# Factorization kernel: the linear layer and the squares' product with outputs on the partitions, four of its outer products by two levels of Strassen in pairs

## The chip, the cores and the metric

The kernel runs on one core of a Trainium2 chip. The metric is the device time of one execution in microseconds (us); less is better. All data are f32.

## The reference

`x` is 1024 x 512, `weight` is 64 x 512 x 512 (e, f, m), `lin_w` is 512 x 512:

```python
out_lin = x @ lin_w.T + lin_b
xv = jnp.einsum('bf,efm->bem', x, weight)
zp = jnp.einsum('bf,efm->bem', jnp.square(x), jnp.square(weight))
interaction = 0.5 * jnp.sum(jnp.square(xv) - zp, axis=1)
return out_lin + interaction
```

The sum over e goes into the second product: the sum of `zp` over e is the product of the squares of `x` (1024 x 512) with the sum over e of the squares of `weight` (512 x 512). It is called the squares' product below. The first product, `xv`, has no such shortcut: it is 64 products of 1024 x 512 with 512 x 512, squared and summed over e.

## The kernel before

**Groups and trees.** The 512 model columns are cut into 16 groups of 32. Within a group the four quadrants of the weights are loaded (w11, w12, w21, w22a or w22b), each 512 columns wide for one quarter of the group's columns and all 64 e. The group's product is done by two levels of Strassen's scheme in Winograd's form: seven outer products, each a `tree` of seven inner ones. A `product` of a tree is two matmuls of 128x512 into one PSUM buffer (b1, b3 or one of two b2). The stationary side are sums of blocks of x, held in `x_all` (X1 to X7, seven slots each); the moving side are blocks of the weights and their sums t1 to t4, which GpSimd makes ahead of each tree. ScalarE copies PSUM to SBUF or from b1 to b2, VectorE adds PSUM to earlier blocks, `finish` squares a block on ScalarE and sums it over e on VectorE (into `acc`). `w_squares` squares the weights on ScalarE and sums them over e on VectorE into `w2_sum`. A group's finished `acc` is halved and stored to DRAM (`acc_dram`).

**The linear layer** comes first: one level of the same scheme, seven products (`lin_product`, `big_product`) of 8 matmuls of 128x256; the batch rows lie on the partitions, x is the stationary side. Its four blocks go to DRAM (`lin_dram`).

**The squares' product** comes last, with one level too: seven products (`zp_product`), x squared as the stationary side, the batch on the partitions. The blocks of x are loaded again, squared on ScalarE, and summed on GpSimd; column sums of `w2_sum` are made on GpSimd (`column_sums`). The bias (broadcast over the partitions), the linear blocks and the groups' sums are loaded and accumulated by DMA into four output blocks, `add_part` adds the products from PSUM with a factor of -0.5, `add_edge` adds the last group's own sums, and each block is stored.

**The order.** `Plan` collects every operation with a cost per engine and what it reads and writes. The order on TensorE is given by keys: a tree s has key 7 s plus a place for each of its products:

```python
PLACE = {5: -6, 3: -2, 1: 0, 6: 3, 2: 4, 7: 6, 4: 9}
```

so that products of three neighbouring trees alternate (in the steady state 1, then 5 of the next tree, 4 of the one before, 6, 2, 3 of the next, 7). From these keys each operation gets a latest time, and `order` runs a list schedule over ScalarE, VectorE, GpSimd and SyncE: an engine takes the ready operation whose latest time comes first, and does not start one that would hold up a more urgent one. Loads and stores are issued by SyncE at most `AHEAD = 50.0` us before their latest time; a DMA is planned with 0.45 us of issue, its `move` time on a shared wire, and 2.0 us to land; GpSimd's accumulating ones with 0.9, a longer move, and 2.5. The result is a fixed order of instructions on each engine; the engines take them in that order and wait for each other by semaphores.

Of the kernel before, what the change touches and what calls it, by code (L numbers as in the profile page):

```python
# [29 lines left out]
class Plan:  # L30
# [10 lines left out]
    AHEAD = 50.0  # L41

# [5 lines left out]
    def add(self, costs, emit, reads=(), writes=(), key=None, land=0.0,  # L48
            move=0.0, both=False):
        op = SimpleNamespace(  # L50
            n=len(self.ops), costs=costs, emit=emit, key=key, land=land, move=move,
            deps=set(), succ=[], latest=None, end=None, both=both, engine=None,
        )
        for r in reads:
            if r in self.writer:
                op.deps.add(self.writer[r])
        for w in writes:
            op.deps.update(self.readers[w])
            if w in self.writer:
                op.deps.add(self.writer[w])  # L60
        for r in reads:
            self.readers[r].append(op.n)
        for w in writes:
            self.writer[w], self.readers[w] = op.n, []
        op.deps.discard(op.n)
        self.ops.append(op)
# [124 lines left out]
def kernel(  # L191
# [33 lines left out]

    nc = tc.nc
    NG, NQ, _, NCB, KH, N = weight.shape
    B = xT.shape[1]
    M = out.shape[1]
# [49 lines left out]
    acc_ring = ring("acc", 2, [P, NB, MG])  # L279
    w2_sum = sb.tile([P, NK, M], F32, tag="w2_sum", name="w2_sum")  # L280
    acc_dram = dram.tile([P, NB, M], F32, tag="accd", name="accd")
    lin_dram = dram.tile([P, NB, M], F32, tag="lind", name="lind")

    plan = Plan()
    engines = {DVE: nc.vector, POOL: nc.gpsimd}
    PAIR = 1.72
# [70 lines left out]
    for at, k in enumerate((2, 3, 0, 1)):  # L357
        load_x(1, k, 0, 2, 10.0 + 0.8 * at)
    nc.scalar.preload_act_table(AF.Square)
# [50 lines left out]
    def quarter(ap):  # L410

        return ap.rearrange("p a (b m) -> p (a b) m", b=2)

# [12 lines left out]
    def big_product(bank, lhs, rhs, first, keys, by_k=False):  # L426

        (a, a_names), (b, b_names) = lhs, rhs
        steps = [(u, [k]) for k in range(KH) for u in range(G)]
        for (u, ks), key in zip(steps if by_k else [(u, range(KH)) for u in range(G)], keys):  # L430
            def emit(_, u=u, ks=ks):
                for j in range(2):
                    for k in ks:
                        nc.tensor.matmul(  # L434
                            buf[bank][:, u, ts(j, HM)],
                            a[:, k, ts(2 * u + j, P)],
                            b[:, k, :],
                            start=first and j == 0 and k == 0,
                            stop=k == KH - 1,
                            skip_group_check=True,  # L440
                        )

            names = a_names + b_names
            if by_k:
                names = sum((a_names[2 * k + u:2 * k + u + 1] + b_names[k:k + 1] for k in ks), ())
            plan.add({PE: PAIR * len(ks) / KH}, emit, names + ((bank, u),), ((bank, u),), key=key)
# [20 lines left out]
    def lin_product(p, bank, first, key, last=None, by_k=False):  # L467
        keys = [key, last or key + 0.2, key + 0.4, key + 0.6]
        big_product(bank, lhs[p], rhs[p], first, keys, by_k)

    def lin_store(n, h, c):
        dma(lin_dram[:, ts(h, NB // 2), ts(c, HM)], quarter(buf[n]), (n,), (("lind", h, c),))

    def lin_last(n, bank, sign):

        def emit(_):
            if sign > 0:
                nc.vector.tensor_add(buf[n], buf[bank], buf[n])
            else:
                nc.vector.scalar_tensor_tensor(  # L480
                    buf[n], buf[n], -1.0, buf[bank], ALU.mult, ALU.subtract
                )

        reads = both_halves(bank) if bank.startswith("b") else (bank,)
        plan.add({DVE: 1.14}, emit, (n, *reads), (n,))

    lin_product(1, "b2_1", True, -1000, by_k=True)
    act(buf["ob2"], buf["b2_1"], None, both_halves("b2_1"), ("ob2",))
# [4 lines left out]
    act(buf["c_0"], buf["b2_0"], None, both_halves("b2_0"), ("c_0",))  # L493
    lin_product(5, "b3", True, -997)
    act(buf["c_1"], buf["b3"], None, both_halves("b3"), ("c_1",))
    lin_product(6, "b2_1", False, -996)
    act(buf["ob3"], buf["b2_1"], None, both_halves("b2_1"), ("ob3",))
    lin_product(3, "b3", False, -995)
    act(buf["c_2"], buf["b3"], None, both_halves("b3"), ("c_2",))
# [19 lines left out]
    def used(*names):  # L519

        plan.add({SP: 0.0}, None, (), names, land=-plan.HOP)

    for n in tuple(a_buf.values()) + ("ob0", "ob1"):
        used(n, *((n, r, u) for r in range(KH) for u in range(2)))
    for b in ("b1", "b3", "b2_0", "b2_1"):
        used(b, *both_halves(b))
# [158 lines left out]
    for g in range(NG):  # L685
# [7 lines left out]
        for idx, i in enumerate(order):  # L693
# [8 lines left out]
            if i == 5:  # L702
                w_squares(g, "w22")
            tree(7 * g + idx, g, i, order)
        if g + 1 < NG:
            names = tuple((acc_name[g], *k) for k in acc_parts)
            a = buf[acc_name[g]]
            plan.add({ACT: 0.4}, lambda _, a=a: nc.scalar.mul(a, a, 0.5), names, names)
            dma(acc_dram[:, :, ts(g, MG)], buf[acc_name[g]], names, names + (("accd", g),), 0.9)


    for n in ("w11", "w12", "T2", w(NG, "w22")):
        for c in range(2):
            buf[n, c] = buf[n][:, c]
        used(n, (n, 0), (n, 1))
    for b in ("b1", "b3", "b2_0", "b2_1"):
        used(b, *both_halves(b))
    last = acc_name[NG - 1]
    blocks = [(h, c) for h in range(2) for c in range(2)]
    lin_all = dict(zip(blocks, ((n, c) for n in ("T2", w(NG, "w22")) for c in range(2))))  # L720
    xe = dict(zip(blocks, ((n, c) for n in ("w11", "w12") for c in range(2))))
    for (h, q), n in xe.items():
        dma(buf[n], x_src[:, ts(q, KH), ts(h, H)], (), (n,))
    edge = {0: HM, 1: HM - MG}
    for h, c in blocks:
        n, rows = lin_all[h, c], ts(h, NB // 2)
        for j in range(NB // 2):
            dma(quarter(buf[n])[:, j, :], lin_b[ts(c, HM)].partition_broadcast(P), (), (n,), 0.5)
        load_more(n, lin_dram[:, rows, ts(c, HM)], (("lind", h, c),), 2.7, quarter)
        load_more(n, acc_dram[:, rows, c * HM:c * HM + edge[c]],  # L730
                  tuple(("accd", x) for x in range(NG - 1)), 2.7,
                  lambda ap, w=edge[c]: quarter(ap)[:, :, 0:w])
    for n in xe.values():
        act(buf[n], buf[n], AF.Square, (n,), (n,), 1.07)

    place = {5: 1, 6: 6, 7: 2, 3: 7}
    lhs = {p: (buf[xe[b]], (xe[b],)) for p, b in ((1, (0, 0)), (2, (0, 1)), (4, (1, 1)))}
    a21 = (buf[xe[1, 0]], (xe[1, 0],))
    for p, a, b, kind in (
        (5, a21, lhs[4], "a + b"),  # L740
        (6, 5, lhs[1], "a - b"),
        (7, lhs[1], a21, "a - b"),
        (3, lhs[2], 6, "a - b"),
    ):
        i = place[p]
        a, b = (lhs[z] if isinstance(z, int) else z for z in (a, b))
        lhs[p] = (block4(i), (f"R{i}",))
        x_sum((f"R{i}", f"X{i}", f"Y{i}"), block4(i), a[0], b[0], kind, a[1] + b[1], 1024, POOL)
    w2_quad = [w2_sum[:, ts(q, KH), ts(c, HM)] for q in range(2) for c in range(2)]
    w2_names = [  # L750
        tuple(("w2", q, m) for m in range(c * HM, (c + 1) * HM, MI))
        for q in range(2) for c in range(2)
    ]
    zt_place = dict(zip(range(1, 5), place.values()))
    zt = {k: x_all[:, i - 1, 4:6, :] for k, i in zt_place.items()}
    zt_names = {k: (f"X{i}", ("zt", k)) for k, i in zt_place.items()}
    column_sums(POOL, w2_quad, zt, w2_names, zt_names)
    rhs = {1: (w2_quad[0], w2_names[0]), 2: (w2_quad[2], w2_names[2]),
           3: (w2_quad[3], w2_names[3])}
    rhs.update({p: (zt[k], zt_names[k][1:]) for p, k in ((4, 4), (5, 1), (6, 2), (7, 3))})  # L760

    def add_edge(h):

        n = lin_all[h, 1]
        l = quarter(buf[n])[:, :, edge[1]:HM]
        a = buf[last][:, ts(h, NB // 2), :]
        plan.add(
            {DVE: 0.3},
            lambda _: nc.vector.scalar_tensor_tensor(l, a, 0.5, l, ALU.mult, ALU.add),
            (n,) + tuple((last, i, pos) for i in ((2, 3), (4, 5))[h] for pos in range(4)), (n,),  # L770
        )

    out_dst = out.rearrange("(n p) m -> p n m", p=P)
    last_key = 7 * (7 * NG - 1) + PLACE[4]
    bank_a, bank_2, bank_b, bank_3 = "b1", "b2_0", "b2_1", "b3"

    def add_part(h, c, bank, store, piece=None):

        n = lin_all[h, c]
        tiles = piece or (0, 4)  # L780
        o = quarter(buf[n])[:, tiles[0]:tiles[1], :]
        b = quarter(buf[bank])[:, 0:tiles[1] - tiles[0], :]
        name = (n, piece) if piece else n
# [81 lines left out]
```

## Time and profile before

| | before |
|---|---|
| median of 3 runs (lowest to highest), us | 1405.06 (1404.98 to 1405.61) |
| profiled execution, us | 1405.08 |
| its span, us | 1403.3 |
| granted TensorE clock | 0.999 |
| TensorE busy, us (share), records | 1398.5 (100%), 3364 |
| VectorE / ScalarE / GpSimd busy, us | 1082.3 / 692.5 / 1037.4 |
| DMA, mean over the span | 141 GB/s |

The span goes from the first to the last instruction of the profiled execution; the execution's own time is 1.8 us longer. PE is TensorE's matmuls, PEld its weight loads, DVE VectorE, ACT ScalarE, POOL GpSimd, SP SyncE; a trailing q is an engine's issuing queue. An f32 matmul leaves two records. L608 is the line of the trees' matmul, L434 that of the linear layer and of the squares' first six products, L820 that of its last.

### The profile page before, as it was taken

What the parts mean: (1) busy time and instruction counts of PE and PEld (TensorE: products, weight loads), DVE (VectorE), ACT (ScalarE), POOL (GpSimd) and SP (SyncE); (2) the same over time, 40 slices, a digit from 0 to 9 for tenths busy, and PEclk for the clock granted to TensorE, in tenths of its full rate; (3) what the DMA queues carried; (4) which work ended last, traced back from release to release, by engine and by line L of the source; (5) the groups of instructions that cost most, each with busy time, mean ns of one, the idle gap of its engine ahead of it and who ended that gap; (6) DMA issues with size and microseconds to landing.
All of it is one profiled execution on the core that took longest, in us unless ns stands there. A gap on an engine that the chain in (4) does not pass through costs nothing.

```text
span 1403.3 us, 10560 instructions
## 1 busy us (share of the span) xinstructions
PE 1398.5 (100%) x3364; PEld 639.8 (46%) x3364; DVE 1082.3 (77%) x934; ACT 692.5 (49%) x719; POOL 1037.4 (74%) x706
## 2 busy tenths in 40 slices
PE   9999999999999999999999999999999999999998
PEld 7444444444444444444444444444444444444446
DVE  7977696867859687696867869687696867869676
ACT  3545463544636355463544636455463544636442
POOL 4796776958678596776958678596777958678694
PEclk9999999999999999999999999999999999999999
DMA  6572562917538183562917548282572907447365
GB/s 228 161 196 75 135 180 77 237 38 186 148 103 200 53 221 91 138 184 77 232 36 188 145 105 198 56 223 85 142 183 79 230 33 191 143 109 198 87 122 118
DMA packets 54551, 197.57 MB, mean 141 GB/s; under 512 B 19168, under 2 KB 30688, under 8 KB 32608
## 3 DMA queue, kind: packets, MB, share of 16 engines
q0 software_dynamic: 15312, 84.81, 31.4%
q1 hardware_dynamic: 38624, 111.55, 22.7%
q8 instruction: 28, 0.46, 0.1%
q10 hardware_dynamic: 560, 0.52, 0.1%
q14 instruction: 27, 0.22, 0.0%
HBM read 173.93 MB, written 6.16 MB: 128 GB/s over the span
## 4 chain that ended last, share of the span: by engine, by line
PE 100%; DVE 0%; issue 0%
PE b L608 96%; PE b L434 3%; PE b L820 0%; PE b L364 0%; DVE w22a L786 0%
## 5 line engine op out<-in xcount | busy, mean ns | idle before, releaser
L608 PE MATMUL b<-t,x_all 128*128 128x512 f32 x1792 | 805.9, 592 | 0.0
L608 PEld LDWEIGHTS b<-t,x_all 128*128 128x128 f32 x1792 | 340.4, 190 | 427.9 <-issue 420.5
L608 PE MATMUL b<-w,x_all 128*128 128x512 f32 x768 | 358.1, 592 | 0.0
L294 POOL TENSOR_TENSOR t<-w 128x512 f32<-128x512 f32 x128 | 173.2, 1354 | 156.1 <-PE b L608 85.0
L306 ACT COPY p<-b 128x1024 f32<-128x1024 f32 x161 | 162.0, 1006 | 161.8 <-PE b L608 161.8
L608 PEld LDWEIGHTS b<-w,x_all 128*128 128x128 f32 x768 | 145.9, 190 | 183.3 <-issue 172.4
L294 POOL TENSOR_TENSOR t<-w,t 128x512 f32<-128x512 f32 x128 | 175.7, 1373 | 61.6 <-PE b L608 61.6
L308 ACT ACTIVATE oa<-oa 128x1024 f32<-128x1024 f32 x124 | 129.7, 1057 | 139.0 <-DVE oa L294 137.1
L608 PE MATMUL b<-T,x_all 128*128 128x512 f32 x384 | 180.4, 592 | 0.0
L315 DVE TENSOR_REDUCE acc<-oa 128x16 f32<-128x1024 f32 x124 | 149.2, 1213 | 37.8 <-ACT oa L308 37.8
L306 ACT COPY b<-b 128x1024 f32<-128x1024 f32 (+1 forms) x114 | 113.1, 992 | 122.9 <-PE b L608 120.1
L315 DVE TENSOR_REDUCE w_sum<-wsq 128x16 f32<-128x1024 f32 x128 | 154.9, 1212 | 20.7 <-ACT wsq L308 20.7
L294 DVE TENSOR_TENSOR oa<-b,p 128x1024 f32<-128x1024 f32 x95 | 116.0, 1221 | 37.7 <-PE b L608 37.6
L294 POOL TENSOR_TENSOR t<-T 128x512 f32<-128x512 f32 x64 | 90.6, 1415 | 58.0 <-issue 33.2
L308 ACT ACTIVATE wsq<-w 128x1024 f32<-128x1024 f32 x96 | 98.1, 1056 | 69.1 <-DVE w_sum L315 69.1
L308 ACT ACTIVATE c<-c 128x1024 f32<-128x1024 f32 x68 | 70.1, 1056 | 93.0 <-POOL c L294 62.2
L608 PEld LDWEIGHTS b<-T,x_all 128*128 128x128 f32 x384 | 73.0, 190 | 91.8 <-issue 91.6
L294 DVE TENSOR_TENSOR ob<-b,p 128x1024 f32<-128x1024 f32 x48 | 58.7, 1222 | 68.2 <-PE b L608 68.2
L294 DVE TENSOR_TENSOR p<-b,p 128x1024 f32<-128x1024 f32 x79 | 96.4, 1220 | 17.5 <-PE b L608 17.4
L294 POOL TENSOR_TENSOR t<-T,t 128x512 f32<-128x512 f32 x64 | 81.3, 1270 | 18.9 <-PE b L608 18.9
L294 POOL TENSOR_TENSOR ob<-ob,p 128x1024 f32<-128x1024 f32 x32 | 89.8, 2815 | 0.0
L294 POOL TENSOR_TENSOR c<-oa,p 128x1024 f32<-128x1024 f32 x32 | 88.6, 2767 | 0.0
(86 smaller groups left out, 1392.8 us busy)
## 6 DMA issues: line engine op xcount, KB each, us to landing
w<-weight SPq DMA_DIRECT2D x48, 1024.0 KB, 4.9
T<-weight POOLq DMA_DIRECT2D x45, 1024.0 KB, 8.6
T<-weight SPq DMA_DIRECT2D x30, 1024.0 KB, 7.1
w<-weight POOLq DMA_DIRECT2D x16, 1024.0 KB, 11.2
w<-T POOLq DMA_DIRECT2D x16, 1024.0 KB, 7.0
w22a<-weight SPq DMA_DIRECT2D x8, 1024.0 KB, 8.1
w22b<-weight SPq DMA_DIRECT2D x8, 1024.0 KB, 8.1
w<-xT SPq DMA_DIRECT2D x4, 512.0 KB, 4.8
```

The source lines that it names most:

```text
L294: f(o, a, b)
L306: nc.scalar.copy(o, i)
L308: nc.scalar.activation(o, i, func)
L315: lambda _: nc.vector.tensor_reduce(o, i.rearrange("p a (m e) -> p a m e", e=E), axis=AX.X, op=ALU.add),
L434: nc.tensor.matmul(buf[bank][:, u, ts(j, HM)], a[:, k, ts(2 * u + j, P)], b[:, k, :], start=first and j == 0 and k == 0, stop=k == KH - 1, ...
L608: nc.tensor.matmul(buf[b][:, j, :], buf[f"X{i}"][:, SLOT[p], ts(j, P)], op, start=first, stop=True, skip_group_check=True,)
```

## The change

1. **Linear layer.** The stationary side are now blocks of `lin_w`, the moving side blocks of x, so that model columns lie on the partitions. The bias becomes a 128x4 tile with one value a partition, and is added when ScalarE copies the products from PSUM (`lin_copy`).
2. **Groups' sums.** A group's `acc` is halved, turned in 32x32 blocks by a VectorE transpose (`turn`) and stored with the model columns on the partitions, by four DMAs (`place`). There is one `acc` buffer instead of two, and one `turned`.
3. **Squares of x.** In groups 1 to 7, one of the seven outer blocks of x squared is made in each (`x_squares`): loads, squares, sums on VectorE, stored to `sq_dram`; for blocks 1, 2, 5 and 6 with the sums of their inner level.
4. **Squares' product.** Outer products 1 and 2, and 5 and 6, are done in pairs by a second level (`twin_tree`): for each of seven inner products, two matmuls of 128x256, one for each member, into the two halves of a PSUM buffer. The first pair stands in the last group's sequence, between its fifth and its sixth tree; the second follows the last tree. Products 4, 7 and 3 stay at one level (`one_level`), on top of an earlier block that ScalarE puts into PSUM (`preload`). Their keys put parts of product 4 between the last tree and the second pair. The last group squares w22 two trees earlier.
5. **End.** Output blocks have model columns on the partitions and are stored in pieces from SyncE or ScalarE; the kernel's output is transposed on the way out (a view). The last group's own sums reach their partitions by DMAs within SBUF before `add_edge`.

The diff, cut to its core:

```diff
-    acc_ring = ring("acc", 2, [P, NB, MG])
+    acc_ring = ring("acc", 1, [P, NB, MG])
+    make("turned", [P, NB, MG])
+    bias = sb.tile([P, M // P], F32, tag="bias", name="bias")
...
+    nc.scalar.dma_start(bias[:], lin_b)
+    landing("bias", 9.5)
...
-    def big_product(bank, lhs, rhs, first, keys, by_k=False):
+    def lin_product(p, bank, first, key, last=None, by_k=False):
+        (a, a_names), (b, b_names) = lhs[p], rhs[p]
+        for at, key in enumerate((key, last or key + 0.2) + (key + 0.4, key + 0.6) * by_k):
+            if by_k:
+                k, u = divmod(at, 2)
+                steps = [(k, c, slice(u * Q, (u + 1) * Q)) for c in range(2)]
...
+            else:
+                steps = [(k, at, slice(0, H)) for k in range(KH)]
...
+                    nc.tensor.matmul(
+                        buf[bank][:, c, rows], b[:, k, ts(c, P)], a[:, k, rows],
...
+    def lin_copy(n, bank, c, sign):
+        for u in range(2):
+            plan.add({ACT: 0.56}, lambda _, u=u: nc.scalar.activation(
+                    buf[n][:, u, :], buf[bank][:, u, :], AF.Identity,
+                    bias=bias[:, 2 * c + u:2 * c + u + 1], scale=sign,
...
+    def turn(g, tiles, half=True):
...
+            plan.add({ACT: 0.2 + 0.25 * size}, lambda _: nc.scalar.mul(a, a, 0.5), row, row)
+        plan.add({DVE: 0.1 + 0.27 * size}, lambda _: nc.vector.transpose(
...
+    def place(dst, b, names, writes, move):
+        rows = dst.rearrange("m (n q b) -> q m n b", q=P // MG, b=MG)
+        for q in range(P // MG):
+            dma(rows[q], buf["turned"][ts(q, MG), b, :], names, (writes + (q,),), move)
+
+    def x_squares(i):
+        a, b = c_ring(), c_ring()
...
+                dma(buf[o], x_src[:, ts(q, KH), ts(h, H)], (), (o,))
+                act(buf[o], buf[o], AF.Square, (o,), (o,), 1.07)
+        one, two, kind = {
+            1: ("A11", None, None), 2: ("A12", None, None), 4: ("A22", None, None),
+            5: ("A21", "A22", "a + b"), 6: (5, "A11", "a - b"), 7: ("A11", "A21", "a - b"),
+            3: ("A12", 6, "a - b"),
+        }[i]
...
+            x_sum((a,), buf[a], buf[a], buf[b], kind, (a, b), 1024)
+        if i in raw_dram:
+            dma(raw_dram[i], buf[a], (a,), (("rawd", i),))
+        slots = sq_dram[:, i - 1, 0:4, :].rearrange("p (k q) b -> p k (q b)", k=2)
+        if i in (3, 4, 7):
+            return dma(slots, buf[a], (a,), (("sqd", i),))
...
+            x_sum(to, o, x, y, kind, (a, b), Q)
...
-            if i == 5:
+            if i == (5 if g < NG - 1 else 2):
                 w_squares(g, "w22")
+            if idx == 1 and 0 < g < 8:
+                x_squares((1, 2, 4, 5, 6, 7, 3)[g - 1])
+            if idx in before:
+                before[idx]()
+            tree(7 * g + idx + sum(idx >= b for b in before), g, i, order)
...
+    def square_load(i):
+        names = (f"R{i}", f"X{i}", f"Y{i}")
+        dma(buf[f"X{i}"], sq_dram[:, i - 1], (("sqd", i),), names, 3.1)
...
+    def twin_tree(at, b2, members):
+        bank = {n: buf[n][:, :, 0:Q] for n in ("b1", "b3", b2)}
...
+        def product(p, b, first):
+            for u, (i, _, _) in enumerate(members):
+                op, names = tt[i][p]
+                plan.add({PE: PAIR / 4}, lambda _, u=u, i=i, op=op: nc.tensor.matmul(
+                        bank[b][:, u], op, buf[f"X{i}"][:, SLOT[p], :], start=first, stop=True,
...
+                    key=7 * at + PLACE[p] + 0.1 * u,
...
+        product(5, "b3", True)
+        aside(5, 3)
+        product(3, "b3", False)
+        aside(3, 1)
+        product(1, "b1", True)
+        act(bank[b2], bank["b1"], None, ("b1",), (b2,), 0.65)
+        product(6, b2, False)
+        to(1, b2, 3)
+        product(2, "b1", False)
+        to(0, "b1")
+        product(7, b2, False)
+        to(3, b2, 5)
+        product(4, b2, False)
+        to(2, b2)
...
+    group(last, {5: first_twins})
...
+            one_level(4, upper[u], u, q * Q, (q + 1) * Q, ((-0.6, -0.4), (9.5, 6.4))[q][u])
...
+    twin_tree(S, b2, ((6, v, u2), (5, None, f)))
+    for h in (1, 0):
+        b, names = turn(last, 1 + h, h == 1)
+        place(buf["oa2"][P - MG:P, h, :], b, names, ("edge", h), 0.0)
     add_edge(1)
...
+        one_level(7, (b2, u), u, 0, H, 11 - u)
...
+            one_level(3, bank, u, q * Q, (q + 1) * Q, 14 - 2 * u + q)
+            collect((0, 1), bank, u, q * Q, (q + 1) * Q)
+        if u:
+            add_edge(0)
+        for q in range(2):
+            store(0, 1, (2 * q + u,))
```

In `twin_tree`, `to` takes an inner product's result out of PSUM (one 128x512 operation for the first pair; one of 128x256 for each member of the second), and `aside` keeps those of b3 in SBUF, with earlier blocks added on GpSimd where a member has them. `S` is 113, the place after the last tree; the first pair has 110, between trees 109 and 111. `first_twins` also starts the loads of the linear blocks and of the groups' sums, and scales `w2_sum` by -0.5 (`halve`).

## The prediction

> **What bounds the kernel now.** I read the page first. TensorE (PE) is busy for 1398.5 of 1403.3 us, VectorE (DVE) 77%, GpSimd (POOL) 74%, ScalarE (ACT) 49%, at a granted clock of 0.999. Then the chain of work that ended last, in order of time:
>
> ```profile
> 3.68 4.52 PE b L434 x16
> 8.20 0.02 issue
> 8.22 19.34 PE b L434 x88
> 27.56 1.72 PE b L608 x4
> 29.27 1.73 PE b L434 x8
> 31.00 1342.43 PE b L608 x3128
> 1373.43 3.45 PE b L434 x16
> 1376.89 1.72 PE b L608 x4
> 1378.60 17.27 PE b L434 x80
> 1395.87 3.47 PE b L820 x16
> 1399.34 0.02 issue
> 1399.36 0.42 DVE w22a L786
> ```
>
> The columns are start, length, what. PE never stands still between 0.78 and 1399.34, so the time is PE's work plus 3.96 us from its last matmul to the end of the span (1403.3). Each f32 matmul leaves two records: 3128 records in 1342.43 us are 0.4292 us each, so a 128x512 matmul of the trees (L608) costs 0.858 us. The last product's three groups (L434 late, L820) are 112 records, 56 matmuls of 256 columns, in 3.45 + 17.27 + 3.47 = 24.19 us: 0.432 us each. Only two things can move the time: fewer columns through PE, or a stop of PE, for which the waits of ACT between 31 and 1372 us show what the present order leaves open:
>
> ```profile
> ACT p L306 <- PE b L608: 159.4, 54, 5.9
> ...
> ACT wsq L308 <- DVE w_sum L315: 69.1, 18, 4.7
> ```
>
> Each line gives who waited for whom, the total, how often, the longest. ACT's list, and DVE's beside it, name no DMA as a releaser at all: the squares of the weights (wsq) are fed by loads, and none came late. The rows of DMA issues (size, median us to landing) price what the change adds:
>
> ```profile
> w<-weight SPq DMA_DIRECT2D x48, 1024.0 KB, 4.9
> ...
> w<-xT SPq DMA_DIRECT2D x4, 512.0 KB, 4.8
> accd<-acc SPq DMA_DIRECT2D x15, 128.0 KB, 6.3
> ...
> out<-w22a SPq DMA_DIRECT2D x2, 128.0 KB, 2.1
> ```
>
> **Part 1: PE's work, on the path.** Before, the seven products of the squares are 56 matmuls of 256 columns, 24.19 us. After, four of them (1, 2, 5, 6) run as two pair trees of 7 products x 2 members, 28 matmuls of 256 columns; products 4 and 3 are 8 such matmuls each; product 7 is 4 matmuls of 512. That is 44 x 0.432 + 4 x 0.858 = 22.44 us, 1.75 us less. In the linear layer the weights become the stationary side; five of its seven products go from 40 matmuls of 256 to 20 of 512: 17.28 - 17.17 = 0.11 us less. The first two keep 16 of 256 and the same loads in the same order, so the beginning (where PE takes 25.59 us for 56 x 0.432 = 24.19) stays. PE: **-1.86 us**, its last matmul at about 1397.5. That is the whole prize: 0.13% of the time.
>
> **Part 2: the linear layer's copies, off the path.** Each 1.01 us ACT copy becomes two halves with bias and scale (the 128x512 copy took 0.57): 1.14. The tightest user is product 3 on b3, which comes one product (3.45 us) after product 5. The bias is 2 KB on ACT's queue behind three loads; the load in front of it was issued at about 2 us and took 6.5, so bias lands near 9, when product 1 has just ended (8.20), and its bank is needed again only after three more products. Cost 0. ACT's in-order queue holds the next copy of x behind that first bias copy, at most 1 us, against over 10 us until the trees use it.
>
> **Part 3: the squares of x, in groups 1 to 7.** Eleven 512 KB loads, 9 squares on ACT (1.06 each), 4 DVE sums of 128x1024 and 16 of 128x256, and 13 stores are moved from the end into the groups, past the queues of SP, ACT and DVE. The DVE prices, alone and beside POOL: a 128x1024 sum took 1.18 us at 13.68 us, where POOL was idle; the groups of DVE sums by shape (busy us, mean ns, idle before) give it beside POOL, and the small one:
>
> ```profile
> L294 DVE TENSOR_TENSOR x_all<-x_all 128x256 f32<-128x256 f32 x8 | 5.4, 687 | 7.3 <-ACT x_all L306 7.3
> ...
> L294 DVE TENSOR_TENSOR T<-w,w 128x1024 f32<-128x1024 f32 x2 | 4.6, 2284 | 0.0
> ```
>
> The dearest group (5 or 6) adds 2.28 + 4 x 0.69 = 5.0 us to a DVE that is busy 64.9 of 84 us a group, and 2.1 to an ACT busy 42.2. Capacity is there; what can hurt is order. ACT and DVE take their instructions in order: an ACT square whose load is late holds every PSUM copy queued behind it. The handover it would break: product 1 ends, ACT copies b1 to b2 (1.0), and product 6 needs it two products (3.43 us) later, so about 2.0 us are free after two hops of 0.2. The order plans 0.45 + 1.75 + 2.0 + 0.3 = 4.5 us for such a load; the nearest row measured 4.8, so 0.3 late, which the 2.0 cover. Lower bound 0: a PE that is never idle has nothing to win back; upper bound, if every one of 11 were 3 us late, 11 x 1.0 = 11 us. I take 0.1, because the row is near the plan and since ACT and DVE never waited for a load.
>
> The turning of each group's sums adds one DVE transpose of 128x256. No row shows one; between the 0.28 of a 128x128 DVE op and the 1.21 of a 128x1024 reduce I take 0.4, in 19 us of idle time a group. Four stores replace one, on SP; behind them stand weight loads that SP issues up to 50 us ahead. Cost 0, and if SP were held, 50 us of lead would have to go first.
>
> **Part 4: the last group.** The squares of w22 come two trees earlier; the first pair tree stands between trees 5 and 4. Its X2 (0.9 MB) can only be loaded once tree 2's last product has gone: five products, 8.58 us, before its first use. 1 MB took 4.9 us in the row above, 8.1 in w22a's row on the page: covered, by 0.5 us in the worse case. In the last pair tree the handovers shrink: product 6 to DVE to product 7 has 0.43 + 0.86 = 1.29 us, and needs 0.2 + 0.42 (a 128x256 DVE add at 1399.36) + 0.1. It fits unless a 1.22 us DVE add stands in front, when it is 0.2 to 0.3 late; the same from 7 to 4. I take 0.1, between 0 and 0.6. POOL loses 4 sums of x (2.46 to 4.36 each at the end) and gains the inner sums (planned 3.3 twice), 8 sums of 128x256 and two asides: about even, and the first half is ready long before.
>
> **Part 5: the end.** Now the last product's DVE add (0.42) and a 128 KB store close the span: 3.96 us after PE. After, the same add and the same store do. New is a chain to the two stores before them: tree 3's last product ends 6 x 0.864 + 3.43 + 3.46 = 12.07 us before PE's end; then DVE add 1.22, square 1.06, reduce 1.21, transpose 0.4, four issues of 0.525 (accd's), the landing, and the edge add, about 0.6: 6.6 us and a landing, with some 2.5 us of hops and of DVE's pair-tree adds in front. The landing of 64 KB in 128-byte pieces lies between 1.8 (fastest 128 KB store) and 5.6 (fastest accd, 128 KB in such pieces); 3 is in between as it is half the bytes. That makes 12.1, just PE's end, so the edge's two stores and the last two crowd: 1.5 MB leave in the last 5 us, at the 342 GB/s of 1400 to 1401 us 4.4 us of transfer. Price 0 to +1.5, also -0.3 if the second issuing queue helps; I take **+0.5**.
>
> The Trainium skill ("DMA: Bandwidth & Descriptors", Why small descriptors are slow) says that the penalty of small pieces belongs to HBM, and that copies within SBUF are spared it. The edge copies are within SBUF, so by the page they would land in about 2 us (Specifications and the fit beside it give 2.0 plus bytes over 436 GB/s, an estimate), and the end would cost 0: 1403.4. No row here shows such a copy; the sum keeps its own bounds.
>
> Sum: 1405.08 (profiled execution; the median of the runs is 1405.06) - 1.86 + 0.1 + 0.1 + 0.5 = **1403.9 us**. Its own range: 1402.7 (end -0.3, no stops) to 1405.6 (end +1.5, stops 0.9).
>
> **Rivals.** *The saving is eaten at the end or in the pair trees* (15%): edge chain at +1.5 and handovers at 0.6: 1405.3. For it: VectorE is busy about 23 of the last 26 us already. Still inside what counts as no change.
>
> *Late loads stop PE* (22%): the eleven loads of Part 3, taken by in-order ACT and DVE, in groups where POOL's accumulating loads (1 MB, 8.6 to 11.2 us) share the wires. It decides from a lateness of 2.0 us. For it: w22a's loads took 8.1 us against 6.2 planned, and a 512 KB transfer of the linear sums up to 11.7. Against: no wait of ACT or DVE on DMA in 1340 us. With half of them 3 us late, 5.5 x 1.0 = 5.5 us: 1409.4, slower than now.
>
> *Much faster* (5%): the end would have to shrink by 1 us more; but 0.42 add, 0.36 issue and 1.8 of landing are in every end: about 1402.0.
>
> *The change does not do what it says*: two levels on four products must show as 3308 PE records instead of 3364 (1568 tree matmuls, 36 linear, 48 squares, 2 warm-up, times two). The code leaves no doubt of it; no chance given.
>
> **How the numbers follow.** The likeliest (58%) is 1403.9. A measurement of this kernel tells a change of about 0.2% (2.8 us) from none: faster below 1402.25, slower above 1407.87. Likeliest and first rival lie within: 0.73; late loads 0.22; much faster 0.05. The range goes from 1402.6 to 1408.6, into the late-load case until some two in ten are left out; the likeliest alone has 1402.7 to 1405.6.
>
> **What would show it.** Right: PE unbroken from 31 us to about 1397.5; 3308 records; 3.9 to 5 us from last matmul to end; no DMA among ACT's releasers in groups 1 to 7. Wrong: waits of PE's weight loads on ACT or DVE between 100 and 690 us that lengthen a group beyond 84.1 us (late loads), a gap between the first and the last pair tree, or an edge add after PE's end.

## The result, and the profile after

| | before | after |
|---|---|---|
| median of 11 runs (lowest to highest), us | 1405.61 (1404.94 to 1406.04) | **1409.2** (1408.49 to 1409.52) |
| profiled execution / span, us | 1405.08 / 1403.3 | 1409.28 / 1407.2 |
| PE's last matmul ends, us | 1399.34 | 1403.20 |
| from there to the end of the span, us | 3.96 | 4.00 |

The ratio is 1.0026, interval 1.0017 to 1.0035: slower, by a little more than the 0.2% that can be told from no change, and 0.6 us above the top of the range. The page of the kernel after:

```profile
PE 1398.1 (99%) x3308; PEld 628.9 (45%) x3308; DVE 1094.7 (78%) x976; ACT 711.8 (51%) x760; POOL 1043.1 (74%) x736
```

The 3308 records are there, so PE got the smaller work. It no longer works without a break. The chain of waits of the kernel after (start, length, what), cut, from 1381.85 us to PE's end:

```profile
1381.85 1.74 PE b L1083 x8
...
1386.24 0.38 ACT b L322
...
1386.67 1.14 PE b L938 x4
...
1388.01 0.76 DVE T L975 x2
...
1388.81 1.13 PE b L938 x4
1389.94 0.88 PE b L1083 x4
...
1390.85 0.77 DVE T L975 x2
...
1391.75 1.10 PE b L938 x4
1392.85 2.59 PE b L1083 x8
...
1395.47 0.60 ACT b L322
...
1396.11 2.00 PE b L1083 x4
...
1400.81 0.34 DVE T L1095
...
1401.19 2.01 PE b L1083 x8
```

L938 is the second pair tree, L1083 the products at one level; line numbers are those of the changed kernel. Where before had PE alone, ScalarE and VectorE now stand between its pieces, five times. PE's waits after 1383 us in the kernel after (who, for whom, total, times, longest); in the kernel before this list is empty:

```profile
PE b L1083 <- DVE T L1095: 1.4, 1, 1.4
PE b L938 <- DVE T L975: 1.1, 2, 0.9
PE b L1083 <- ACT b L322: 0.7, 1, 0.7
PE b L938 <- ACT b L322: 0.5, 1, 0.5
```

In order of time PE waits 0.52 us before product 6 of the pair tree (1386.67), 0.15 before 7 (1388.81), 0.94 before 4 (1391.75), 0.68 before the second half of outer product 7 (1396.11) and 1.37 before the last half of outer product 3 (1401.19): 3.7 us. Each time the next group is slow as well: the one at 1386.67 took 1.14 us for two matmuls of 256 columns, where the same work in an unbroken run took 0.86. Five times about 0.27 us are 1.4 more. A count of the work agrees: from 1383.41 PE had 22 matmuls of 256 columns and 6 of 512 left, 22 x 0.432 + 6 x 0.858 = 14.65 us, to 1398.06. It ended at 1403.20: **5.1 us of stops**. The expectations below count each stop from where PE at full speed would have been done with what it had, and so call the five 0.68, 0.42, 1.2, 0.84 and 1.54 us.

The timeline of the kernel after (start, busy time, operation, and in brackets the idle time before it with its releaser) shows what kind of waits these are:

```profile
1392.69 2.74 PE L1083 MATMUL b<-x_all,w 128*128 128x256 f32 x8
...
1396.11 1.98 PE L1083 MATMUL b<-x_all,w 128*128 128x512 f32 x4 [0.68 <-ACT b L322]
...
1398.19 0.69 DVE L1095 TENSOR_TENSOR w22a<-w22a,b 128x512 f32<-128x512 f32 x1 [2.14 <-PE b L1083]
```

The first half of outer product 7 was in its bank by 1395.44 (end of the group at 1392.85 in the chain). VectorE, idle for 2.14 us, adds it at 1398.19: only after the second half, in the other bank of the same buffer, has ended too (1398.11).

### The profile page after: what moved, and what is told of

Its sections match the earlier page's. It is cut to its first block, busy times and chain, and to the rows that moved or that the text cites. A ratio compares the mean times of both kernels' runs of the same rounds, so it can differ in the third digit from the quotient of the medians.

```text
span 1407.2 us, 10698 instructions
## 1 busy us (share of the span) xinstructions
PE 1398.1 (99%) x3308; PEld 628.9 (45%) x3308; DVE 1094.7 (78%) x976; ACT 711.8 (51%) x760; POOL 1043.1 (74%) x736
## 4 chain that ended last, share of the span: by engine, by line
PE 98%; DMA 1%; DVE 0%; ACT 0%; issue 0%; ACTq 0%; SPq 0%; DVEq 0%
PE b L623 96%; PE b L456 1%; PE b L938 1%; PE b L1083 1%; DMA oa<-xT 0%; DMA ob<-lin_wT 0%; ACT b L322 0%; DVE T L975 0%; DVE w22a L1095 0%; ACT T L322 0%; DVE x_all L310 0%; ACTq L356 0%; DVE T L1095 0%; SPq L349 0%; ACT ob L324 0%
## 5 line engine op out<-in xcount | busy, mean ns | idle before, releaser
L310 POOL TENSOR_TENSOR t<-w,t 128x512 f32<-128x512 f32 x128 | 176.4, 1378 | 60.4 <-PE b L623 60.4
L310 POOL TENSOR_TENSOR t<-T 128x512 f32<-128x512 f32 x64 | 90.3, 1411 | 56.6 <-issue 33.2
L324 ACT ACTIVATE c<-c 128x1024 f32<-128x1024 f32 x77 | 79.4, 1057 | 77.5 <-POOL c L310 51.7
```

The lines of the kernel that those rows point to most:

```text
L310: f(o, a, b)
L324: nc.scalar.activation(o, i, func)
```

## The experiments

**The theory:** an engine that reads one half of a PSUM buffer waits for every matmul or copy that was issued earlier into any part of that buffer, and one that writes a half waits for the earlier reads too. The plan that sets the order gives the halves names of their own (`(b, u)`, `upper`) and takes them to be independent; the semaphores, which are made from the order of the instructions, go by the whole buffer. **The rival:** ScalarE and VectorE have too much to do in the last 25 us. A third question is the first 31 us, where the kernel after is 0.5 us behind.

**1. The wait by itself.** A small kernel of its own with four cases: VectorE copies what one matmul wrote, while other matmuls go to another place. A tile is a buffer; the second number of `mm` is how many matmuls, the third their columns (512 where it is left out).

```python
    # one tile, two banks: the read of bank 0 is issued after the matmuls to bank 1
    mm(one[:, 0, :], 1)
    mm(one[:, 1, :], 6)
    nc.vector.tensor_copy(o["one"][:], one[:, 0, :])
    # two tiles
    mm(twoa[:], 1)
    mm(twob[:], 6)
    nc.vector.tensor_copy(o["two"][:], twoa[:])
    # one bank, lower and upper half
    mm(low[:, 0:256], 1, 256)
    mm(low[:, 256:512], 12, 256)
    nc.vector.tensor_copy(o["low"][:, 0:256], low[:, 0:256])
    # one tile, two banks: the read of bank 0 comes first in the program
    mm(pre[:, 0, :], 1)
    nc.vector.tensor_copy(o["pre"][:], pre[:, 0, :])
    mm(pre[:, 1, :], 6)
...
```

> A kernel that computes nothing of the reference: it measures one wait by itself. VectorE reads a PSUM half that one matmul wrote, while six more matmuls (about 5.1 us at 0.858 each) run into another half. Four cases: other half of the same two-bank tile, a tile of its own, other half of the same bank, and the read placed before the six in the program. Theory (waits go by whole PSUM tiles): in the first and third case the read starts only after the six matmuls, some 5 us late; with a tile of its own it starts about 0.2 us after its matmul; in the fourth case the six matmuls start only after the read (0.5 to 0.7 us of PE standing). Rival (waits go by halves, and the stops at the end come from late engines): the read starts 0.2 us after its own matmul in all cases and PE never stands.

Its timeline (a matmul has two records):

```profile
12.33 6.17 PE L29 MATMUL one<-a 128*128 128x512 f32 x14
...
18.34 1.02 PE L29 MATMUL twoa<-a 128*128 128x512 f32 x2
...
18.54 0.69 DVE L35 COPY oone<-one 128x512 f32<-128x512 f32 x1 [18.54 <-PE one L29]
...
19.40 0.69 DVE L39 COPY otwo<-twoa 128x512 f32<-128x512 f32 x1 [0.17 <-PE twoa L29]
...
24.35 5.78 PE L29 MATMUL low<-a 128*128 128x256 f32 x26
...
30.16 0.42 DVE L43 COPY olow<-low 128x256 f32<-128x256 f32 x1 [10.07 <-PE low L29]
...
31.77 5.42 PE L29 MATMUL pre<-a 128*128 128x512 f32 x12 [0.78 <-DVE opre L46]
```

In one buffer the copy waits for all seven matmuls (18.54), though its own, the first, was done six matmuls (about 5.1 us) earlier. With a buffer for each bank it starts at 19.40, when its own matmul (twoa) has just ended, and the six to twob run on beside it. With the copy issued first, it is PE that stands, 0.78 us, until a bank has been read that it doesn't write. The two halves of one bank behave like the first case: the copy of the lower half starts at 30.16, when the matmuls to the upper half have ended. All four are as the theory has them.

**2. Product 4 out of the pair tree's buffer.** The one-level product 4 has its quarters in the upper columns of `b2`, whose lower columns the pair tree uses. They go to `b3`, which is free by then, and the pair tree is handed to the plan ahead of them.

```diff
-    upper = {u: (b2, u, "upper") for u in range(2)}
+    twin_tree(S, b2, ((6, v, u2), (5, None, f)))
+    upper = {u: ("b3", u, "upper") for u in range(2)}
...
-    twin_tree(S, b2, ((6, v, u2), (5, None, f)))
```

> Only the four pieces of product 4 are moved: from the upper halves of the second pair tree's own b2 to the upper halves of b3, which the pair tree has left by then. Theory (waits by whole PSUM tiles): PE's stops before the pair tree's products 6 (0.68 us) and 4 (1.2 us) go or shrink to 0.3 together, since ACT's preloads and product 4's third piece no longer lie between the pair tree's writes and reads of b2; the stops before product 7 (0.4), before the second half of product 7 of the outer level (0.84) and before the last half of product 3 (1.5) stay: about 1.5 us less, 1407.7. Rival (ACT and DVE are merely too busy at the end): no change, 1409.2.

1407.62 us (1407.4 to 1408.37), ratio to the kernel before 1.0014 (1.0004 to 1.0024): 1.6 us less than after, as expected. Product 4's matmuls lose here the block that ScalarE had put into the bank: by the Trainium skill ("PSUM — Partial Sum Buffer", The four PSUM rules) the first matmul of a group clears the accumulation marks of its whole bank, and a later one that only adds overwrites where the mark is clear. No trace shows these marks; the operations and their sizes are as in the kernel after. PE's waits after 1383 us in this kernel (who, for whom, total, times, longest):

```profile
PE b L1083 <- DVE T L1095: 1.4, 1, 1.4
PE b L1083 <- ACT b L322: 0.7, 1, 0.7
PE b L938 <- DVE T L975: 0.2, 1, 0.2
```

The pair tree's stops fell to 0.2 us; those in products 7 and 3, which were not touched, stayed at 0.7 and 1.4. ScalarE and VectorE have as much to do as in the kernel after (busy for 9.1 and 12.9 us between 1383 and 1404 us, there for 9.3 and 12.6), so it was not their load that held the pair tree.

**3. Products 7 and 3 in buffers of their own.** The complement: product 4 as in the change, the halves of 7 and the quarters of 3 spread over different buffers.

```diff
-    for u in (1, 0):
-        preload((b2, u), u2, u, 0, H)
+    seven = {1: (b2, 1), 0: ("b3", 0)}
+    for u in (1, 0):
+        preload(seven[u], u2, u, 0, H)
...
-        for q, bank in enumerate((("b3", u), ("b1", u))):
+        for q, bank in enumerate(((("b1", 1), (twin_b2, 1)), ((b2, 0), ("b3", 1)))[1 - u]):
```

> Only the buffers of the outer products 7 and 3 are changed: the halves of product 7 lie in b2 and b3 instead of both in b2, and the four pieces of product 3 in b1, the pair tree's b2, the other b2 and b3, so that no two neighbours share a tile. Theory (waits by whole PSUM tiles): the stop before product 7's second half (0.84 us) and the one before product 3's last half (1.5 us) go: 2.2 us less, 1407.0. Rival (ACT and DVE too busy at the end): no change, 1409.2.

1408.34 us (1407.97 to 1408.85), ratio 1.0018 (1.0009 to 1.0028): 0.9 less, where 2.2 was expected. (Here too some of these products overwrite a preloaded block.) The stop of 1.5 us before product 3's last half went; 0.59 of the 0.68 us of waiting before 7's second half stayed: the ScalarE copy that puts the earlier block there no longer waits for the first half, as it did in the kernel after (0.48 us), but stands behind other copies on ScalarE's own queue. In this stop the rival has a part. PE ended at about 1401.7, but the span went on 5.0 us instead of 4.0. The chain of waits of this kernel says why:

```profile
1398.23 2.46 DMA oa<-turned
...
1400.92 0.09 DVE T L1052
```

The last group's sums land at 1400.68, and the edge add (L1052) stands with the last adds: the cost that the prediction had put at the end, which the stops had hidden in the kernel after.

**4. Less work for ScalarE and VectorE at the end.** The squares and sums of the last tree's four blocks are left out.

```diff
+        if g == NG - 1 and i == 3:
+            return
         act(buf[n], buf[n], AF.Square, (n,), (n,), 1.07)
```

> Left out: squaring and summing of the last tree's four blocks (four ACT squares of 1.06 us and four DVE sums of 1.21 us in the last 25 us), so the last group's sums lack a quarter. Buffers as in the changed kernel. Rival theory (ACT and DVE too busy at the end): PE's stops after 1383 us (about 5 us) mostly go, 1405 or less. Theory (waits by whole PSUM tiles): only what a square in front of a copy costs goes, the 0.7 us before product 6 at most; 1408.5 to 1409.

1416.3 us (1415.64 to 1419.02), ratio 1.0078 (1.0063 to 1.0093): slower by 7 us, which neither theory had said. With those sums gone, the plan turned part of the group's sums earlier and copied it into a buffer that the trees still used: the copies were issued from 1343.66 and landed at 1351.93, VectorE's next add into that buffer waited 8.5 us for them, and PE 4.6 us for VectorE, to 1354.56. Behind it the clock granted to PE was 0.50 from 1355 to 1358 us. By 1359 PE was 6.4 us behind the kernel after. As a time this run decides nothing. In the tail the wait before product 6 went: in the kernel after a square of the last tree stood in front of the copies for it on ScalarE's queue. The waits for VectorE stayed (0.94, 0.97 and 1.38 us), though VectorE and ScalarE had only 8.1 and 6.4 us to do from 1389 to 1411 us, where the kernel after had 12.6 and 9.3 from 1383 to 1405. That speaks against the rival.

**5. The bias load moved behind the loads of x.** For the beginning: in the kernel after, SP needs 3.03 us for its first five issues (2.29 before), with the small bias load on ScalarE's queue beside them.

```diff
-    nc.scalar.dma_start(bias[:], lin_b)
-    landing("bias", 9.5)
+    nc.sync.dma_start(bias[:], lin_b)
+    landing("bias", 12.0)
```

> Only the bias load is changed: issued by SP behind all loads of x instead of by ACT among them, and planned to land at 12.0 us instead of 9.5. In the changed kernel SP's first five loads took 3.03 us to issue (2.29 before) while ACT issued the bias, and the first tree matmul came at 28.08 us (27.56 before). Theory (the bias load, 128 pieces of 16 bytes, holds SP's issues): SP's five are back at 2.3 us, the first tree matmul is at 27.5 to 27.7, and 0.5 to 0.7 us are won: 1408.6. Rival (the loads' arrival merely varies, or the swapped roles of x and lin_w cost it): no change, 1409.2.

1409.27 us (1409.04 to 1409.53), ratio 1.0025 (1.0015 to 1.0035): no change. The issues were back at 2.29 us, but x landed no earlier: PE waited 0.77 us for it at 7.32, and its first tree matmul came at 28.38, later than after's 28.08.

**6. The pair tree with neighbours in buffers of their own throughout.** Product 4's quarters in the upper columns of `b1` and `b3`, the halves of 7 in two different `b2`, product 3 spread over three; 4 and 3 start fresh where the preload was.

```diff
+    upper = {(x, u): (x, u, "upper") for x in ("b1", "b3") for u in range(2)}
...
+    twin_b2, b2 = b2, b2_ring()
+    seven = {1: (b2, 1), 0: (twin_b2, 0)}
```

> The last pair tree stays, but no two neighbours on PE share a PSUM tile: product 4's four pieces go to the upper halves of b3 and b1 as fillers between the pair tree's products 2, 7, 4 (sums on DVE instead of ACT's preload and copy), product 7's halves to two different tiles, product 3's pieces to b1, b3, b2, b1 with the earlier block added on GpSimd. Theory (waits by whole PSUM tiles): of the 5.15 us of PE's stops after 1383 us at most 0.8 stay (before product 7, whose two members still share a tile); the edge's DMA and the stores then set the end, as with own tiles for 7 and 3 alone, some 0.7 us more behind PE's last matmul: 1405.5. Rival (ACT and DVE too busy at the end; DVE has even more to do here): 1408 or more.

1406.73 us (1406.23 to 1408.55), ratio 1.0008 (0.9999 to 1.0017): 2.5 us less than after, and no longer to be told from before. PE's waits after 1383 us:

```profile
PE b L623 <- DVE ob L310: 0.5, 1, 0.5
PE b L1083 <- DVE T L975: 0.3, 1, 0.3
```

PE ended at 1399.49, 3.7 us earlier than after, with 0.8 us of waits instead of 3.7, although VectorE was busier than there (14.8 us between 1383 and 1404, there 12.6). That the rival does not allow for VectorE; ScalarE had less to do than there (5.2 us, 9.3), since the preloads are gone. The span (1404.7) goes on for 5.2 us more: the edge add starts at 1399.54, behind another add on VectorE's queue, and the last two VectorE adds stand behind it. So 1.2 us of the gain were given back at the end.

**7. The last pair at one level.** Products 6, 5 and 4 at one level; the halves of 5, 4 and 7 lie in different buffers, those of 6, with other products in between, in the two banks of `b3`. The first pair tree stays. That gives up 23.23 - 22.44 = 0.8 us of the saving (14 + 4 + 4 matmuls of 256 and 16 of 512) for fewer handovers.

> The second pair is undone: products 5 and 6 at one level, 8 matmuls of 128x512 instead of 28 / 2 = 14 of 128x256, so PE has 6.87 - 6.05 = 0.82 us more to do, but every handover has at least two products of 1.72 us between; neighbours lie in different PSUM tiles. The first pair, the linear layer and all else stay. Theory (waits by whole PSUM tiles at short distance): PE's stops after 1383 us fall from 5.15 to 0.5 or less; with the end 0.7 us longer behind PE: 1409.2 - 4.65 + 0.82 + 0.7 = 1406.1. Rival (the order's ACT and DVE work is too much): 1408 or more.

1405.84 us (1405.51 to 1406.36), ratio 1.0 (0.9991 to 1.0009). One stop was left, from PE's waits after 1383 us:

```profile
PE b L1086 <- ACT b L322: 1.1, 1, 1.1
```

It stands before product 7's first half, in one bank of a `b2`, and waits for a copy of product 3's sum into the other bank of the same `b2`: the theory's wait again, put in by my own choice of banks. Here, where PE stops, the end is short: 3.85 us from PE's last matmul (1400.35) to 1404.2.

**8. That stop taken out.** The first half of product 3 becomes one bank of 512 columns, so that no copy into that buffer comes ahead of product 7.

```diff
-        for q, bank in enumerate(((("b3", 0), (bB, 0)), (("b1", 1), ("b3", 1)))[1 - u]):
+    three = {1: ((("b3", 0), 0, H),), 0: ((("b1", 1), 0, Q), ((bB, 0), Q, H))}
...
+        for bank, lo, hi in three[u]:
```

> The kernel of the last run (last pair at one level, 1405.84 us), with the first half of product 3 as one bank of 512 columns where it was two pieces of 256, so that no copy into the second PSUM tile of the ring is queued between product 4 and product 7. Theory (a matmul waits for whatever was issued earlier to the other half of its PSUM tile): PE stood 1.06 us before product 7 on a copy of product 3's sum into that tile's other half; that stop goes, and 4 matmuls of 512 columns replace 8 of 256 (3.43 for 3.46 us). PE's last matmul at about 1399.1, 4.0 us from there to the end if the edge's add is done by then: 1404.8 us. Rival (ScalarE is simply too busy in the last 20 us): a stop of about 1 us remains before product 7 or before product 3, 1405.8 us.

1405.31 us (1405.02 to 1405.49), 0.9998 of before (0.999 to 1.0007; before in these runs 1405.39). The chain of waits of this kernel:

```profile
1384.87 1.72 PE b L623 x4
1386.59 12.04 PE b L1086 x32
1398.63 0.01 issue
1398.64 0.04 DVE T L1098
```

PE is unbroken again to 1398.63, 0.7 us earlier than before; its list of waits after 1383 us is empty. ScalarE and VectorE have nearly as much to do in this stretch as in the kernel after (8.1 and 11.5 us between 1383 and 1404, there 9.3 and 12.6): with experiments 2 and 6 the rival is out, but for the square in front of product 6 (experiment 4) and the queue in front of 7's second half (experiment 3). But the span ends 4.7 us later, not 4.0. The edge add (1397.92, after 0.31 us of waiting for its DMA) is in front of the last two adds, so VectorE is done 0.76 us after PE, before 0.44; and the last stores of 128 KB land in 2.4 to 2.5 us, before in 2.1, with the DMA engines full from 1399 to 1401 us (360 and 343 GB/s; before too, with 342). The 0.7 us won on PE are lost there. This version equals before and beats the change by 3.9 us (3.7 when each is taken against before in the same runs); no version was faster than before.

**9. The bias load in the kernel before.** The same 2 KB on ScalarE's queue, used by nobody.

```diff
+    spare = sb.tile([P, M // P], F32, tag="spare", name="spare")
+    nc.scalar.dma_start(spare[:], lin_b.rearrange("(p a) -> p a", p=P))
     nc.scalar.preload_act_table(AF.Square)
```

> The kernel before, with nothing changed but a 2 KB load of the bias added on ScalarE's queue after its three loads of the linear weights; what it loads is used by nobody. Theory (the bias load delays the issue of x, and with it the first products): SP's first five issues take about 3.0 us as in the kernel after, for 2.29 before, TensorE's first tree matmul comes about 0.5 us after 27.56, and the time is 1406.3 us against 1405.8. Rival (the landing of the first loads varies from launch to launch): the issues may lengthen, but the first tree matmul lies anywhere from 27.5 to 28.5 and the time stays at 1405.8 us.

1405.46 us (1405.22 to 1406.3), ratio 1.0001 (0.9992 to 1.001). SP's five issues took 3.05 us, so the load does slow them. The chain of waits of this kernel:

```profile
3.68 24.22 PE b L436 x104
27.91 1.72 PE b L610 x4
```

The first tree matmul comes 0.35 us later than in the one profile of before, and the time does not show it.

## Why the prediction was wrong, step by step

- **Part 1, PE's work: right.** 3308 records; in experiment 8, whose plan differs only in the tail, PE needs 0.8 us less from its first tree matmul on, for 0.97 by the same rule.
- **Part 1, "the beginning stays": off by 0.6 us in the profile.** The trees' long run starts at 31.51 instead of 31.00, and the 0.11 us of the linear layer are not to be seen. In the profile of the kernel after the loss is one wait of PE, 0.66 us at 15.80, for VectorE's sum of a block of x that had landed at 14.39; the kernel before has no such wait. In profiles of eight kernels with the changed linear layer the first tree matmul came between 27.68 and 28.45 us, in two with the old one at 27.56 and 27.91. The bias load lengthens SP's issues, but neither experiment 5 nor 9 moved the time. Whether the rest is the new order of operands or the loads' varying arrival stays open; the linear layer alone wasn't tried.
- **Parts 2 and 3: right.** The eleven loads, the squares and the sums are covered; the nine of the loads that the page lists together landed in 5.4 us (median), where 4.8 was taken, and the margin of 2.0 held. ACT's waits from 31 to 1372 us after, for whom, name no DMA, and neither do DVE's:

```profile
ACT p L322 <- PE b L623: 157.0, 54, 5.9
...
ACT wsq L324 <- DVE w_sum L331: 68.8, 20, 4.7
```

  PE runs from 31.51 to about 1383 us unbroken. The rival of late loads, at 1409.4 close to the time that came, is refuted: near it for another reason.
- **Part 4, the handovers of the last pair tree: the step that failed.** It said 0.1, between 0 and 0.6, from "0.2 + 0.42 + 0.1" in 1.29 us. Measured: 5.1 us of stops. Of the two handovers that it priced, 6 to 7 cost 0.4 us (0.15 of it waiting), inside the bounds; 7 to 4 cost 1.2. With the stop before 6 (0.7) that makes 2.3 us inside the pair tree, of which experiment 2 removes 1.6 by taking product 4 out of its buffer. The others lie between the halves of products 7 and 3, which the step did not look at and so put at nothing: experiment 3 removes the one before the last half of 3, while the one before the second half of 7 stays there at 0.59 and is gone only in 6 and 8, where ScalarE has less to do as well. The sum took the halves of a buffer for independent, as the plan's names do. With the wait by buffer, a handover from 6 to 7 contains both members' matmuls, both members' VectorE adds (0.76 us for the two) and whatever product 4 has in the buffer's upper columns. It is this last that cost most: without it, 0.2 us of waiting is left in the pair tree. The operations' own durations were right.
- **Part 5, the end: 0.04 instead of 0.5 in the kernel after**, because the stops let the edge overtake. Where they are gone the price appears: 5.0, 5.2 and 4.7 us from PE's end in experiments 3, 6 and 8, against 3.96, so +0.7 to +1.2, inside its bounds of 0 to 1.5. The landing, taken at 3 us, was shorter. The DMA issues of the kernel after (operation, queue, number, KB each, median us to landing) between 1390 us and the end:

```profile
oa<-turned SPq DMA_DIRECT2D x4, 16.0 KB, 1.8
```

  That agrees with the about 2 us that the prediction took from a page of the Trainium skill ("DMA: Bandwidth & Descriptors"), though the fit stands there under Anatomy of one DMA — SWDGE (gpsimd) path, for copies that GpSimd issues, and these are SP's; one of them took 2.46 in experiment 3. What lengthens the end differs: in experiment 3 the chain goes through issues of 0.59 us each and that landing to the edge add; in 6 and 8 the edge add stands in front of the last adds on VectorE's queue, and VectorE ends 1.5 and 0.8 us after PE, before 0.4.
- **The sum, redone.** In the profiles: 1405.08 - 1.86 (work) + 0.6 (beginning) + 5.1 (stops) = 1408.9, and the profiled execution took 1409.28; 0.3 us of the rest lie outside the span (2.1 us instead of 1.8). One bound of the prediction was added up wrongly: by its own terms the likeliest case begins at 1405.08 - 1.86 - 0.3 = 1402.9, not 1402.7. That changes nothing here, where the time lies above.
- **The rivals.** *Eaten at the end or in the pair trees* had about the right place and too small a price: 0.6 us of handovers. Its signs are not what is seen: the gaps lie inside the last pair tree and behind it, not between the first pair tree and the last, and in the kernel after the edge add (1401.50) comes before PE's end. Its reason was misread too: VectorE is busy in the kernel before for 14.9 us between 1378 and 1404, not for about 23 of 26. As to where a saving goes once the stops are out it was right: in experiments 6 and 8 it ends up in the last microseconds. What the change with both pair trees and no stop at all would take no run shows.

## What to carry to other kernels

When a change puts more, smaller pieces into a PSUM buffer, look at what the waits go by, not at what the plan calls the pieces. Where they go by buffer, as here, two pieces that should overlap belong in two buffers, and every copy into a buffer that is issued ahead of a matmul holds that matmul, whichever bank it writes. A saving of 0.13% on an engine that never waits is worth only as much as the last microseconds let through; sum up the end (adds queued behind one another, issues, bytes against the DMA rate) before counting it. Before taking a predicted time that came true as proof of its mechanism, look for the mechanism's own sign: here the late-load rival had the time almost exactly and nothing of it in the trace.

## What the runs showed of the hardware

- A stop costs PE more than the wait: a group of two 256-column matmuls took 1.14 us after one (1386.67) and 0.86 without (1373.25, same kernel): 0.28 us more. After a wait of 4.6 us (experiment 4) the granted clock fell to 0.50, and two matmuls of 512 columns took 3.43 us, for 1.72 in an unbroken run.
- A 2 KB load issued on ScalarE's queue lengthened five issues on SP beside it from 2.29 to 3.05 us (experiment 9), without any use of its data.
- A VectorE transpose of 128x128 in 32x32 blocks took 0.30 us, and the ScalarE copy of 128x512 with a bias 0.69 where a plain one took 0.57. In the kernel after neither stands in the chain that ended last.
- Two halves of one bank may not be free to overlap even with finer waits: the Trainium skill ("PSUM — Partial Sum Buffer", PSUM bank collisions raise a hardware error) tells to guard PSUM by bank and 32-partition quadrant, or simply by bank. No run here takes such a wait away; what the experiments separated were buffers. By that rule only the waits between two banks of one buffer are needless.
